# Addend rows through VectorE's block transpose and two GpSimd DMAs, and a layer norm behind the last division, in a two-layer graph network kernel

## The chip, the cores and the metric

One core of one Trainium2 chip. The metric is the device time of one execution in microseconds (us). A time below is a median of runs with the range beside it. All runs told here are of the fast state. The profiled span of a run is 1.7 to 1.9 us shorter than its time (1.86 in the profiled run of the kernel before, 1.76 after), so spans are compared with spans.

## The reference, cut to what matters

64 graphs of 256 nodes with 256 features pass two layers. In the first, each graph goes twice through graph attention, then a layer norm, a feed-forward with 1024 hidden columns and another layer norm:

```python
def _gat(h, adj, W, a, out_features):
    Wh = jnp.matmul(h, W)
    Wh1 = jnp.matmul(Wh, a[:out_features])
    Wh2 = jnp.matmul(Wh, a[out_features:])
    e = Wh1 + jnp.swapaxes(Wh2, 1, 2)
    e = jax.nn.leaky_relu(e, negative_slope=ALPHA)
    scores = jnp.where(adj > 0, e, NEG)
    att = jax.nn.softmax(scores, axis=1)
    return jnp.matmul(att, Wh)
# first layer:  h = _gat(x, adj, W1, a1); h = _gat(h, adj, W2, a2)
#               h = ln(x + h);  ln(h + relu(h @ w_ff1 + b_ff1) @ w_ff2 + b_ff2)
# second layer: 8-head attention with relations, @ Wo + bo, ln(src + .), gelu feed-forward, ln
```

The kernel keeps scores transposed, so `Wh1`, one number per node, is needed as a row that every one of the 128 partitions holds. These are the *addend rows*; four belong to each pair of graphs and layer: two graphs, each with exp(Wh1) and exp(0.2 Wh1).

## The kernel before

Graphs go in 32 pairs. Each pair's work is a generator, and a small scheduler interleaves up to three of them. A `yield us, later, needs` says how long the step was, after how many further us of the scheduler's time the next may follow, and which resource that needs. This sets only the order in which instructions are emitted. The build then re-orders within each engine, so the order on the chip is read from the trace.

```python
def addends(y, at, layer, pair, b):
    ...  # rise = exp(Wh1), exp(0.2 Wh1); ratio = exp(-0.8 Wh2): three ScalarE exponentials a graph
def gat_weights(y, at, rise, ratio, adjT, empty, b):
    p = bank()
    for n in range(4):
        col = rise[:, n // 2, n % 2:n % 2 + 1]
        nc.tensor.transpose(p[:, n * P:(n + 1) * P], col.to_broadcast([P, P]), ident)      # L225
    up = work.tile([P, N], F32, name="up", bufs=2)
    nc.scalar.activation(up, p[:, :N], AF.Copy)                                            # L227
    ...
        nc.vector.scalar_tensor_tensor(e[:, j], p[:, N:], ratio[:, j:j + 1], up, ...)      # L232
        nc.vector.scalar_tensor_tensor(e[:, j], adjT[:, k], empty[:, k:k + 1], e[:, j], ...)  # L233
    nc.vector.reciprocal(rs, sums)
    ...  # ScalarE scales xw by rs (L238)

def attention(y, pair, adjT):
    ...
    def into_rows(b):         # output projection of graph b, reads oT (L427)
        ...
        add_rows(y, ps, b)
        layernorm(y, ln[2], b)
    ...
    for n, (b, c) in enumerate(groups):   # 4 groups: 2 graphs x 2 halves of the heads
        ...
        divided(b, c, po)     # reciprocal of the sums (L416), product into oT (L420)
        yield 3.1 if last else 4.1, 4.8 if last else 0.8, None
        ...
        if n == 2:
            into_rows(0)
            yield 1.75, 0.0, None
    into_rows(1)
```

A layer norm runs on VectorE with one power operation on GpSimd (L302).

Of the kernel before, what the change touches and what calls it, by code (L numbers as in the profile page):

```python
# [29 lines left out]
def two_layers(ctx: ExitStack, tc: tile.TileContext, t: dict, out: bass.AP, flag: bass.AP):  # L30
# [25 lines left out]
    def load(pair):  # L56
        rows = slice(2 * pair, 2 * pair + 2)
        xT = io.tile([P, KC, 512], F32, name="xT")
        nc.sync.dma_start(xT, t["xT"][pair].rearrange("(c p) b n -> p c (b n)", p=P))
        adjT = io.tile([P, 4, N], I32, name="adjT", bufs=4)  # L60
        nc.sync.dma_start(adjT, t["adjT"][rows].rearrange("b (c p) n -> p (b c) n", p=P))
        x = io.tile([P, 4, D], F32, name="x", bufs=4)
        nc.sync.dma_start(x, t["x"][rows].rearrange("b (c p) d -> p (b c) d", p=P))
        return xT, adjT, x

# [8 lines left out]
    nc.vector.memset(ones, 1.0)  # L74
    reach = const.tile([P, NPAIR, 2 * KC], F32, name="reach")
    most = const.tile([P, NPAIR, 4], F32, name="most")
    steep = const.tile([P, NPAIR, 4], F32, name="steep")

    def weights(name, pool=const):
        w = t[name]  # L80
# [62 lines left out]

    work = ctx.enter_context(tc.tile_pool(name="work", bufs=1))
    small = ctx.enter_context(tc.tile_pool(name="small", bufs=6))
    psum = ctx.enter_context(tc.tile_pool(name="psum", bufs=8, space=bass.MemoryType.PSUM))

    def bank():
        return psum.tile([P, 512], F32, name="ps")
# [53 lines left out]
    def of_graph(b):  # L203
        return slice(2 * b, 2 * b + 2)


    def addends(y, at, layer, pair, b):


        k = of_graph(b)  # L210
        nc.vector.tensor_reduce(steep[:, pair, 2 * layer + b:2 * layer + b + 1], y[:, k, at:at + 2], axis=AX.XY,  # L211
                                op=ALU.max, apply_absolute_value=True)
        e1, e2 = y[:, k, at], y[:, k, at + 1]
        rise, ratio = small.tile([P, 2, 2], F32, name="rise"), small.tile([P, 2], F32, name="ratio")
        nc.scalar.activation(rise[:, 0], e1, AF.Exp, bias=shift[:, 0:1])  # L215
        nc.scalar.activation(rise[:, 1], e1, AF.Exp, bias=shift[:, 0:1], scale=ALPHA)
        nc.scalar.activation(ratio, e2, AF.Exp, scale=ALPHA - 1.0)
        return rise, ratio

    def gat_weights(y, at, rise, ratio, adjT, empty, b):  # L220

        p = bank()
        for n in range(4):
            col = rise[:, n // 2, n % 2:n % 2 + 1]
            nc.tensor.transpose(p[:, n * P:(n + 1) * P], col.to_broadcast([P, P]), ident)  # L225
        up = work.tile([P, N], F32, name="up", bufs=2)
        nc.scalar.activation(up, p[:, :N], AF.Copy)  # L227
        e = work.tile([P, 2, N], F32, name="e", bufs=4)
        sums, rs = small.tile([P, 2], F32, name="sums"), small.tile([P, 2], F32, name="rs")
        for j in range(2):  # L230
            k = 2 * b + j
            nc.vector.scalar_tensor_tensor(e[:, j], p[:, N:], ratio[:, j:j + 1], up, op0=ALU.mult, op1=ALU.max)  # L232
            nc.vector.scalar_tensor_tensor(e[:, j], adjT[:, k], empty[:, k:k + 1], e[:, j],  # L233
                                           op0=ALU.max, op1=ALU.min, accum_out=sums[:, j:j + 1])
        nc.vector.reciprocal(rs, sums)
        for j in range(2):
            k = 2 * b + j
            nc.scalar.activation(y[:, k, :at], y[:, k, :at], AF.Copy, scale=rs[:, j:j + 1])  # L238
        return e

    def gat_layers(pair, xT, adjT, x):
        nc.vector.tensor_reduce(most[:, pair], adjT.bitcast(U32), axis=AX.X, op=ALU.max)
        empty = small.tile([P, 4], F32, name="empty")
        nc.vector.tensor_scalar(empty, most[:, pair], 0.0, EVEN, ALU.is_le, ALU.mult)
        y = work.tile([P, 4, D + 4], F32, name="xw", bufs=2)
        z = work.tile([P, 4, D + 4], F32, name="xw", bufs=2)
        a, e = [], []
        for b in range(2):
            for j in range(2):
                k = 2 * b + j  # L250
                ps = bank()
                for c in range(KC):
                    nc.tensor.matmul(ps[:, :D + 4], lhsT=xT[:, c, k * P:(k + 1) * P], rhs=w12[:, c],  # L253
                                     start=c == 0, stop=c == KC - 1)
                nc.scalar.activation(y[:, k], ps[:, :D + 4], AF.Copy)
            a.append(addends(y, D + 2, 0, pair, b))
            yield 1.75, b * 1.6, None
        if pair + 1 < NPAIR:
            loaded[pair + 1] = load(pair + 1)
        for b in range(2):  # L260
            e.append(gat_weights(y, D + 2, *a.pop(0), adjT, empty, b))
            yield 0.5, b * 4.4, None
        for b in range(2):
            for i in range(2):
                ps = bank()
                for j in range(2):
                    nc.tensor.matmul(ps[:, :D + 2], lhsT=e[b][:, j, i * P:(i + 1) * P], rhs=y[:, 2 * b + j, :D + 2],  # L267
                                     start=j == 0, stop=j == 1)
                nc.scalar.activation(z[:, 2 * b + i, :D + 2], ps[:, :D + 2], AF.Copy)  # L269
            a.append(addends(z, D, 1, pair, b))  # L270
            yield 1.75, 0.4 + b * 0.6, None
        for b in range(2):
            e.append(gat_weights(z, D, *a.pop(0), adjT, empty, b))
            yield 0.5, b * 4.4, None
        for b in range(2):
            ps = bank()
            for i in range(2):
                for j in range(2):
                    nc.tensor.matmul(ps[:, i * D:(i + 1) * D], lhsT=e[2 + b][:, j, i * P:(i + 1) * P],  # L279
                                     rhs=z[:, 2 * b + j, :D], start=j == 0, stop=j == 1)  # L280
            add_rows(x, ps, b)
            layernorm(x, ln[0], b)
            if b == 0:
                yield 1.75, 0.4, None
        done_with("gat")
        yield 1.75, 6.0, None
# [80 lines left out]
    def attention(y, pair, adjT):  # L367
# [54 lines left out]
        def into_rows(b):  # L422
            ps = bank()
            for j in range(2):
                k = 2 * b + j
                for c in range(KC):
                    nc.tensor.matmul(ps[:, j * D:(j + 1) * D], lhsT=oT[:, c, k * P:(k + 1) * P], rhs=wo[:, c, :],  # L427
                                     start=c == 0, stop=c == KC - 1)
            add_rows(y, ps, b)
            layernorm(y, ln[2], b)  # L430

        groups = [(b, c) for b in range(2) for c in range(KC)]
        v = values_tile()
# [12 lines left out]
        for n, (b, c) in enumerate(groups):  # L446
            last = n == len(groups) - 1
            if not last:
                ahead = scores(*groups[n + 1])
            po = bank()  # L450
            sums(e, po)
            products(c, 0, v, e, po)
            products(c, 1, v, ms, po)
            if not last:
                e, ms = ahead, of_relation_1(groups[n + 1][0], ahead)
            divided(b, c, po)
            yield 3.1 if last else 4.1, 4.8 if last else 0.8, None
            if n == 0:
                following = values_tile()
                for jc in range(2):  # L460
                    values(following, jc, N + jc * P, yT)
                    yield 1.72, 0.0, None
            if n == 1:
                v = following
            if n == 2:
                into_rows(0)
                yield 1.75, 0.0, None
        into_rows(1)
        done_with("attention")
        yield 1.75, 6.0, None  # L470

    def whole_way(pair):
        yield 0.0, 0.0, "gat"
        xT, adjT, x = loaded.pop(pair)
        yield from gat_layers(pair, xT, adjT, x)
        if pair == 0:
            relieve(ff0[1], ff0[0], ln[0][2])
        yield from feed_forward(x, ff0, AF.Relu, ln[1])
        yield 3.44, 6.0, None
        if pair == 0:  # L480
            relieve_attention(ln[1][2])
        yield from attention(x, pair, adjT)
        if pair == 0:
            relieve(ff1[1], ff1[0], ln[2][2])
        yield from feed_forward(x, ff1, AF.Gelu, ln[3])
        nc.sync.dma_start(out[2 * pair:2 * pair + 2].rearrange("b (c p) d -> p (b c) d", p=P), x)
        yield 3.44, 0.0, None

    in_turn((whole_way(pair) for pair in range(NPAIR)), 3)


    ranges = ((reach, NPAIR * 4, N * SAFE), (most, NPAIR * 4, 1.0), (steep, NPAIR * 4, STEEP))
    count = const.tile([P, len(ranges)], F32, name="count")
    for n, (found, width, most_allowed) in enumerate(ranges):
        kept = const.tile([P, width], F32, name=f"kept{n}")
# [434 lines left out]
```

## Time and profile before

| | before |
|---|---|
| time, median of 3 runs (range) | 3386.12 us (3384.53 to 3388.64) |
| profiled span | 3384.70 us |
| start: span's begin to the first feed-forward matmul | 51.43 us |
| middle: from there to the end of the last matmul | 3324.25 us |
| end: after the last matmul | 9.02 us |

I split the span at two points of TensorE's (PE's) timeline because each stretch has another limit. In the start there is one pair and nobody to fill PE's gaps. In the middle, three pairs are interleaved and PE is the bound. At the end everybody waits for the last layer norm and the last store. The views of this kernel are in the prediction.

### The profile page before, as it was taken

What the parts mean: (1) busy time and instruction counts of PE and PEld (TensorE: products, weight loads), DVE (VectorE), ACT (ScalarE), POOL (GpSimd) and SP (SyncE); (2) the same over time, 40 slices, a digit from 0 to 9 for tenths busy, and PEclk for the clock granted to TensorE, in tenths of its full rate; (3) what the DMA queues carried; (4) which work ended last, traced back from release to release, by engine and by line L of the source; (5) the groups of instructions that cost most, each with busy time, mean ns of one, the idle gap of its engine ahead of it and who ended that gap; (6) DMA issues with size and microseconds to landing.
All of it is one profiled execution on the core that took longest, in us unless ns stands there. A gap on an engine that the chain in (4) does not pass through costs nothing.

```text
span 3384.7 us, 46922 instructions
## 1 busy us (share of the span) xinstructions
PE 3335.3 (99%) x18782; PEld 2161.4 (64%) x18782; DVE 1863.3 (55%) x4833; ACT 1366.4 (40%) x2576; POOL 202.8 (6%) x262
## 2 busy tenths in 40 slices
PE   7999999999999999999999999999999999999998
PEld 5656755765676667557656756676576567665755
DVE  5646556556555555565466556555564565565454
ACT  3234434532353254245433542542354335425332
POOL 0000000000000000000000000000000000000000
PEclk9999999999999999999999999999999999999999
DMA  5000100100010001001000100010010001000000
GB/s 170 7 7 26 38 7 9 43 19 13 15 42 14 7 26 38 7 7 44 19 7 13 38 26 7 26 38 7 7 44 19 7 14 38 20 7 19 13 1 14
DMA packets 67296, 78.19 MB, mean 23 GB/s; under 512 B 3712, under 2 KB 58112, under 8 KB 67072
## 3 DMA queue, kind: packets, MB, share of 16 engines
q1 hardware_dynamic: 67072, 75.13, 7.2%
q8 instruction: 150, 2.46, 0.3%
q14 instruction: 74, 0.61, 0.1%
HBM read 58.34 MB, written 16.78 MB: 22 GB/s over the span
## 4 chain that ended last, share of the span: by engine, by line
PE 95%; ACT 4%; DMA 1%; SPq 0%; issue 0%; DVE 0%; POOL 0%; POOLq 0%; DVEq 0%
PE ps L341 26%; PE ps L330 25%; PE ps L364 7%; PE ps L410 7%; PE ps L357 6%; PE ps L382 4%; PE ps L403 4%; PE ps L253 3%; PE ps L427 3%; PE ps L279 3%; PE ps L317 3%; PE ps L267 2%; ACT L215 2%; PE ps L225 1%; ACT L333 1%; ACT xw L269 1%
## 5 line engine op out<-in xcount | busy, mean ns | idle before, releaser
L319 ACT ACTIVATE yT<-ps 128x512 f32<-128x512 f32 x192 | 113.0, 589 | 1069.7 <-PE ps L317 1069.6
L330 PE MATMUL ps<-yT,w_L_gnn_w_ff 128*128 128x512 f32 x1024 | 480.0, 601 | 0.7 <-ACT yT L319 0.7
L330 PE MATMUL ps<-yT,w_L_gnn_W 128*128 128x512 f32 x1024 | 472.4, 596 | 1.4 <-ACT yT L319 1.4
L341 PE MATMUL ps<-w_L_gnn_w_ff,ff 128*128 128x256 f32 x2048 | 458.2, 381 | 0.0
L341 PE MATMUL ps<-w_L_gnn_W,ff 128*128 128x256 f32 x2048 | 456.8, 380 | 0.0
L341 PEld LDWEIGHTS ps<-w_L_gnn_W,ff 128*128 128x128 f32 x2048 | 388.2, 190 | 65.8 <-issue 14.6
L341 PEld LDWEIGHTS ps<-w_L_gnn_w_ff,ff 128*128 128x128 f32 x2048 | 388.1, 190 | 65.8 <-issue 14.3
L396 DVE TENSOR_TENSOR m<-a,adjT 128x512 f32<-128x512 f32 x512 | 327.2, 687 | 175.4 <-ACT a L387 130.3
L302 POOL TENSOR_TENSOR rstd<-rstd,mhalf 128x2 f32<-128x2 f32 x256 | 202.1, 789 | 3175.3 <-DVE rstd L301 3161.6
L387 ACT ACTIVATE a<-ps 128x512 f32<-128x512 f32 x512 | 264.3, 603 | 232.9 <-PE ps L382 232.8
L359 DVE TENSOR_TENSOR v<-ps,b_L_gnn_bv 128x512 f32<-128x512 f32 x128 | 88.1, 689 | 464.4 <-PE ps L357 464.4
L292 DVE TENSOR_TENSOR x<-ps,x 128x512 f32<-128x512 f32 x256 | 175.8, 687 | 265.2 <-PE ps L341 142.1
L333 ACT ACTIVATE ff<-ps,c_L_gnn_b_ff 128x512 f32<-128x512 f32 x256 | 175.9, 687 | 346.0 <-PE ps L330 346.0
L330 PEld LDWEIGHTS ps<-yT,w_L_gnn_W 128*128 128x128 f32 x1024 | 185.3, 190 | 179.0 <-issue 173.7
L330 PEld LDWEIGHTS ps<-yT,w_L_gnn_w_ff 128*128 128x128 f32 x1024 | 182.1, 190 | 178.9 <-issue 175.9
L333 ACT ACTIVATE ff<-ps,c_L_gnn_b 128x512 f32<-128x512 f32 x256 | 175.7, 686 | 148.3 <-PE ps L330 146.7
L357 PE MATMUL ps<-wv,yT 128*128 128x512 f32 x512 | 235.4, 592 | 0.0
L416 DVE RECIPROCAL s<-ps 128x256 f32<-128x256 f32 x128 | 224.0, 1750 | 0.0
L232 DVE SCALAR_TENSOR_TENSOR e<-ps,ratio,up 128x256 f32<-128x256 f32 x256 | 115.8, 475 | 174.0 <-ACT up L227 174.0
L299 DVE BATCH_NORM_STATS2 st<-x 128x6 f32<-128x256 f32 x512 | 192.7, 418 | 8.7
L357 PEld LDWEIGHTS ps<-wv,yT 128*128 128x128 f32 x512 | 97.3, 190 | 122.4 <-issue 122.4
L211 DVE TENSOR_REDUCE steep<-xw 128x1 f32<-128x4 f32 x128 | 19.7, 155 | 256.8 <-ACT xw L269 211.0
(96 smaller groups left out, 4027.6 us busy)
## 6 DMA issues: line engine op xcount, KB each, us to landing
xT<-in_xT SPq DMA_DIRECT2D x32, 512.0 KB, 4.6
adjT<-in_adjT SPq DMA_DIRECT2D x32, 512.0 KB, 3.8
x<-in_x SPq DMA_DIRECT2D x32, 512.0 KB, 4.2
out<-x SPq DMA_DIRECT2D x32, 512.0 KB, 3.2
w_L_gnn_w_ff<-in_L_gnn_w_ff SPq DMA_DIRECT2D x2, 1024.0 KB, 9.4
w_L_gnn_W<-in_L_gnn_W SPq DMA_DIRECT2D x2, 1024.0 KB, 10.3
wv<-in_L_gnn_Wv SPq DMA_DIRECT2D x2, 256.0 KB, 5.0
w_L_gnn_W1T<-in_L_gnn_W1T SPq DMA_DIRECT2D x1, 256.0 KB, 2.8
```

The lines of the kernel that those rows point to most:

```text
L292: nc.vector.tensor_tensor(rows, p, rows, ALU.add)
L299: nc.vector.bn_stats(st[:, j, :], r[:, 2 * b + j, :])
L302: nc.gpsimd.tensor_tensor(rstd, rstd, mhalf[:, :2], ALU.pow)
L330: nc.tensor.matmul(p1, lhsT=w1[:, c, m * P:(m + 1) * P], rhs=yT[:, c, :], start=c == 0, stop=c == KC - 1)
L333: nc.scalar.activation(h, p1, func, bias=b1[:, m:m + 1])
L341: nc.tensor.matmul(p2[:, j * D:(j + 1) * D], lhsT=f[m][:, k * P:(k + 1) * P], rhs=w2[:, m, :], start=m == 0, stop=m == NF - 1)
L357: nc.tensor.matmul(ps, lhsT=yT[:, c, at:at + P], rhs=wv[:, c].rearrange("p r m -> p (r m)"), start=c == 0, stop=c == KC - 1)
L364: nc.tensor.matmul(ps, lhsT=w[:, d, c * P:(c + 1) * P], rhs=yT[:, d, :], start=d == 0, stop=d == KC - 1)
L387: nc.scalar.activation(a, ps[o], AF.Exp)
L396: nc.vector.tensor_tensor(m, a, adj, ALU.mult)
L410: nc.tensor.matmul(po[o * DH:(o + 1) * DH, :N], lhsT=v[:, jc, at:at + DH], rhs=ms[o][:, jc * N:(jc + 1) * N], start=r == 0 and jc == 0, st ...
L416: nc.vector.reciprocal(s, po[:, N:])
```

## The change

Its intent is to take 512 transposes off PE, the bounding engine. VectorE transposes the exponentials in blocks of 32x32 instead, a small DMA writes the blocks to DRAM as rows, and a second DMA broadcasts the rows to all partitions. Both DMAs are issued by GpSimd. In addition the first graph's layer norm behind attention is emitted after the last division rather than before it, the next pair's load and the store come later, and `x` has five buffers instead of four.

```diff
-    def addends(y, at, layer, pair, b):
+    def addends(y, at, layer, pair):
 ...
+        rise, ratio = rises[layer], small.tile([P, 4], F32, name="ratio")
+        of_kind = rise.rearrange("p j (n s) -> p n j s", n=4)[:, :, :, 0]
 ...
+        blocks = small.tile([P, 2, 32], F32, name="blocks")
+        nc.vector.transpose(blocks.rearrange("p j c -> p (j c)"), rise.rearrange("p j c -> p (j c)"))
+        row = scratch.tile([2, 16, 32], F32, name="row")
+        nc.gpsimd.dma_start(row.rearrange("j q c -> q j c"), blocks[0:P:8])
+        rows = work.tile([P, 8, 4, 32], F32, name="rows")
+        nc.gpsimd.dma_start(rows.rearrange("p q n c -> p (q n c)"), row.rearrange("j q c -> (j q c)").partition_broadcast(P))
 ...
-    def gat_weights(y, at, rise, ratio, adjT, empty, b):
-        p = bank()
-        for n in range(4):
-            col = rise[:, n // 2, n % 2:n % 2 + 1]
-            nc.tensor.transpose(p[:, n * P:(n + 1) * P], col.to_broadcast([P, P]), ident)
-        up = work.tile([P, N], F32, name="up", bufs=2)
-        nc.scalar.activation(up, p[:, :N], AF.Copy)
 ...
+        rows, ratio = addends(y, D + 2, 0, pair)
+        yield 1.75, 8.6, None
+        e = [gat_weights(y, D + 2, rows, ratio, adjT, empty, b) for b in range(2)]
+        yield 0.0, 4.6, None
 ...                                   (the same for the second layer; the load of the next pair moved behind it)
             add_rows(y, ps, b)
-            layernorm(y, ln[2], b)
 ...
             divided(b, c, po)
+            if last:
+                layernorm(y, ln[2], 0)
 ...
         into_rows(1)
+        layernorm(y, ln[2], 1)
```

More of the change, by code (lines that the diff above doesn't have):

```diff
@@ L61, in load @@
         nc.sync.dma_start(adjT, t["adjT"][rows].rearrange("b (c p) n -> p (b c) n", p=P))
-        x = io.tile([P, 4, D], F32, name="x", bufs=4)
+        x = io.tile([P, 4, D], F32, name="x", bufs=5)
         nc.sync.dma_start(x, t["x"][rows].rearrange("b (c p) d -> p (b c) d", p=P))
@@ L76, in two_layers @@
     most = const.tile([P, NPAIR, 4], F32, name="most")
-    steep = const.tile([P, NPAIR, 4], F32, name="steep")
+    steep = const.tile([P, NPAIR, 2], F32, name="steep")
+    rises = [const.tile([P, 2, 32], F32, name=f"rise{n}") for n in range(2)]
+    for rise in rises:
+        nc.vector.memset(rise, 0.0)
     def weights(name, pool=const):
@@ L145, in two_layers @@
     small = ctx.enter_context(tc.tile_pool(name="small", bufs=6))
+    scratch = ctx.enter_context(tc.tile_pool(name="scratch", bufs=4, space=bass.MemoryType.DRAM))
     psum = ctx.enter_context(tc.tile_pool(name="psum", bufs=8, space=bass.MemoryType.PSUM))
@@ L204, in of_graph, with gat_weights @@
         return slice(2 * b, 2 * b + 2)
-    def addends(y, at, layer, pair, b):
-        k = of_graph(b)
-        nc.vector.tensor_reduce(steep[:, pair, 2 * layer + b:2 * layer + b + 1], y[:, k, at:at + 2], axis=AX.XY,
-                                op=ALU.max, apply_absolute_value=True)
-        e1, e2 = y[:, k, at], y[:, k, at + 1]
-        rise, ratio = small.tile([P, 2, 2], F32, name="rise"), small.tile([P, 2], F32, name="ratio")
-        nc.scalar.activation(rise[:, 0], e1, AF.Exp, bias=shift[:, 0:1])
-        nc.scalar.activation(rise[:, 1], e1, AF.Exp, bias=shift[:, 0:1], scale=ALPHA)
-        nc.scalar.activation(ratio, e2, AF.Exp, scale=ALPHA - 1.0)
-        return rise, ratio
-    def gat_weights(y, at, rise, ratio, adjT, empty, b):
-        p = bank()
-        for n in range(4):
-            col = rise[:, n // 2, n % 2:n % 2 + 1]
-            nc.tensor.transpose(p[:, n * P:(n + 1) * P], col.to_broadcast([P, P]), ident)
-        up = work.tile([P, N], F32, name="up", bufs=2)
-        nc.scalar.activation(up, p[:, :N], AF.Copy)
+    def addends(y, at, layer, pair):
+        nc.vector.tensor_reduce(steep[:, pair, layer:layer + 1], y[:, :, at:at + 2], axis=AX.XY, op=ALU.max,
+                                apply_absolute_value=True)
+        rise, ratio = rises[layer], small.tile([P, 4], F32, name="ratio")
+        of_kind = rise.rearrange("p j (n s) -> p n j s", n=4)[:, :, :, 0]
+        for b in range(2):
+            e1 = y[:, of_graph(b), at]
+            nc.scalar.activation(of_kind[:, 2 * b], e1, AF.Exp, bias=shift[:, 0:1])
+            nc.scalar.activation(of_kind[:, 2 * b + 1], e1, AF.Exp, bias=shift[:, 0:1], scale=ALPHA)
+        nc.scalar.activation(ratio, y[:, :, at + 1], AF.Exp, scale=ALPHA - 1.0)
+        blocks = small.tile([P, 2, 32], F32, name="blocks")
[4 more added lines that the diff above has]
+        nc.gpsimd.dma_start(rows.rearrange("p q n c -> p (q n c)"), row.rearrange("j q c -> (j q c)").partition_broadcast(P))
+        return rows, ratio
+    def gat_weights(y, at, rows, ratio, adjT, empty, b):
         e = work.tile([P, 2, N], F32, name="e", bufs=4)
@@ L231, in gat_weights @@
             k = 2 * b + j
-            nc.vector.scalar_tensor_tensor(e[:, j], p[:, N:], ratio[:, j:j + 1], up, op0=ALU.mult, op1=ALU.max)
+            nc.vector.scalar_tensor_tensor(e[:, j].rearrange("p (q c) -> p q c", q=8), rows[:, :, 2 * b + 1],
+                                           ratio[:, k:k + 1], rows[:, :, 2 * b], op0=ALU.mult, op1=ALU.max)
             nc.vector.scalar_tensor_tensor(e[:, j], adjT[:, k], empty[:, k:k + 1], e[:, j],
@@ L246, in gat_layers @@
         z = work.tile([P, 4, D + 4], F32, name="xw", bufs=2)
-        a, e = [], []
         for b in range(2):
@@ L255, in gat_layers @@
                 nc.scalar.activation(y[:, k], ps[:, :D + 4], AF.Copy)
-            a.append(addends(y, D + 2, 0, pair, b))
-            yield 1.75, b * 1.6, None
-        if pair + 1 < NPAIR:
-            loaded[pair + 1] = load(pair + 1)
-        for b in range(2):
-            e.append(gat_weights(y, D + 2, *a.pop(0), adjT, empty, b))
-            yield 0.5, b * 4.4, None
+            if b == 0:
+                yield 1.75, 0.0, None
+        rows, ratio = addends(y, D + 2, 0, pair)
+        yield 1.75, 8.6, None
+        e = [gat_weights(y, D + 2, rows, ratio, adjT, empty, b) for b in range(2)]
+        yield 0.0, 4.6, None
         for b in range(2):
@@ L269, in gat_layers @@
                 nc.scalar.activation(z[:, 2 * b + i, :D + 2], ps[:, :D + 2], AF.Copy)
-            a.append(addends(z, D, 1, pair, b))
-            yield 1.75, 0.4 + b * 0.6, None
-        for b in range(2):
-            e.append(gat_weights(z, D, *a.pop(0), adjT, empty, b))
-            yield 0.5, b * 4.4, None
+            if b == 0:
+                yield 1.75, 0.4, None
+        rows, ratio = addends(z, D, 1, pair)
+        if pair + 1 < NPAIR:
+            loaded[pair + 1] = load(pair + 1)
+        yield 1.75, 8.6, None
+        e += [gat_weights(z, D, rows, ratio, adjT, empty, b) for b in range(2)]
+        yield 0.0, 4.6, None
         for b in range(2):
@@ L485, in whole_way @@
         yield from feed_forward(x, ff1, AF.Gelu, ln[3])
+        yield 3.44, 5.0, None
         nc.sync.dma_start(out[2 * pair:2 * pair + 2].rearrange("b (c p) d -> p (b c) d", p=P), x)
-        yield 3.44, 0.0, None
     in_turn((whole_way(pair) for pair in range(NPAIR)), 3)
-    ranges = ((reach, NPAIR * 4, N * SAFE), (most, NPAIR * 4, 1.0), (steep, NPAIR * 4, STEEP))
+    ranges = ((reach, NPAIR * 4, N * SAFE), (most, NPAIR * 4, 1.0), (steep, NPAIR * 2, STEEP))
     count = const.tile([P, len(ranges)], F32, name="count")
```

## The prediction

> **What bounds the kernel now.** I read the page's busy shares first, then the chain that ended last, then TensorE's (PE's) groups by shape, its waits, and timelines of the middle, the start and the end.
>
> ```profile
> PE 3335.3 (99%) x18782; PEld 2161.4 (64%) x18782; DVE 1863.3 (55%) x4833; ACT 1366.4 (40%) x2576; POOL 202.8 (6%) x262
> ...
> PE 95%; ACT 4%; DMA 1%; SPq 0%; issue 0%; DVE 0%; POOL 0%; POOLq 0%; DVEq 0%
> ```
>
> PE is busy 3335.3 of 3384.7 us, so it has 49.4 us of idle time. The chain that ended last is 95% PE. VectorE is 55% and ScalarE 40% busy. So a change gains what it takes out of PE's stream, plus what it takes out of those 49.4 us, and no more.
>
> The row that the change removes, from PE's groups by shape (busy, mean ns of one | idle before):
>
> ```profile
> L225 PE MATMUL ps<-ident,rise 128*128 128x128 f32 x512 | 71.3, 275 | 19.4 <-ACT rise L215 19.4
> ```
>
> These are the transposes that spread the addend rows over all partitions. 275 ns is not what one costs. In the chain, in order of time (start, us, what), from a busy stretch of the middle:
>
> ```profile
> 1011.06 1.72 PE ps L330 x4
> 1012.78 0.87 PE ps L225 x8
> 1013.65 5.15 PE ps L330 x12
> ```
>
> Eight take 0.87 us of the stream, 109 ns each; the row's 275 is the modelled length of an overlapped instruction. So the transposes hold 512 x 0.109 = 55.8 us. PE's waits complete the account:
>
> ```profile
> PE ps L225 <- ACT rise L215: 19.4, 23, 0.9
> PE pw L117 <- DVE junk L111: 7.3, 1, 7.3
> PE ps L253 <- DMA xT<-in_xT: 5.1, 1, 5.1
> PE ps L279 <- ACT xw L238: 3.3, 1, 3.3
> PE ps L267 <- ACT xw L238: 2.6, 1, 2.6
> ```
>
> The largest wait also belongs to L225: the second graph's transposes find their exponentials unfinished in 23 cases. The idle time counts from a modelled end; one wait in the timeline near the end shows what it costs:
>
> ```profile
> 3169.11 0.60 PE L225 MATMUL ps<-ident,rise 128*128 128x128 f32 x4
> 3170.63 0.65 PE L225 MATMUL ps<-ident,rise 128*128 128x128 f32 x4 [0.92 <-ACT rise L215]
> ```
>
> The stream stood from 3169.11 + 4 x 0.109 = 3169.55 to 3170.63, that is 1.08 us where the note says 0.92. 23 x 0.16 = 3.7 us more makes the waits about 23 us. The other listed waits are single and at the start; from about 52 us on PE idles only before L225. The remainder, 3384.7 - 3375.7 = 9 us, is the final layer norm, store and range check after the last matmul.
>
> **What the Trainium skill says.** (1) "Perfetto Trace Analysis", section Identifying the Most-Contended Engine: matmul occupancy misleads because matmuls are pipelined. The trace agrees: 275 ns recorded, 109 ns of stream. (2) "VectorE: DVE Perf Modes", section The three transpose paths: VectorE transposes 32x32 blocks only, so a row of 256 comes out in pieces, and DMAs must join and broadcast them. No transpose on VectorE is in this trace. (3) "DMA: Bandwidth & Descriptors", section Anatomy of one DMA — SWDGE (gpsimd) path: about 2.0 us plus bytes over 436 GB/s; by it (an estimate) the 512 KB broadcast takes 3.2 us. Here no DMA is issued by GpSimd; SyncE's of 512 KB land in 3.2 us (out) to 4.6 us (xT). I use 4 us. (4) Same page, section Two DMAs through the same engine are not ordered: the issuing engine must wait for the first DMA's semaphore before the second. So GpSimd's queue stands still between the two. No run yet shows it.
>
> **The change part by part.**
>
> *Transposes and row copies out.* PE loses 55.8 us of stream and the 23 us of waits. ScalarE loses L227 (128 x 379 ns = 42 us) and some exponentials: per layer and pair five activations instead of six. Neither is on the path. Four PSUM-bank uses per pair go too, and PE waits for none today.
>
> *Addend rows in.* Per layer and pair (64 times): one 128x64 VectorE transpose (estimate 0.2 us, from 0.16 us for the small VectorE operations here and 0.42 for 256 columns), a DMA of 16 blocks x 256 B to DRAM, and a 512 KB broadcast back. The L232 operations stay 256, reading SBUF instead of PSUM; L233, same size and from SBUF, takes 477 ns against 475, so nothing changes. VectorE gains 64 x 0.2 = 13 us and loses 64 reductions of 155 ns = 10 us. The added traffic, 64 x 0.5 MB = 34 MB, is 10 GB/s beside 23.
>
> *Latency.* From the last projection: copy 0.4, four exponentials 1.2 (a table load of 1.28 in some cases), transpose 0.2, first DMA with GpSimd's issue about 3, second about 4.5: 9 to 11 us. Then VectorE needs 2 x (0.48 + 0.48 + 0.08) = 2.1 us a graph and ScalarE 2 x 0.5 us before the product.
>
> I stepped the source's scheduler with the diff's yields, for the order of instructions only. Its delays are 8.6 + 4.6 us, and its steady order puts between 15 and 35 of its microseconds, nearly all of them other pairs' PE work, between the end of the projections and the product. So the latency is covered, with 4 us or more to spare. GpSimd's held queue can delay one layer norm per pair (power at L302) by some 2 us, but its reader, a PE transpose, comes 4 to 8 us later. I allow 2 us in all.
>
> *The start.* Pair 0 has nobody beside it:
>
> ```profile
> 15.35 0.62 PE L225 MATMUL ps<-ident,rise 128*128 128x128 f32 x4
> 16.28 0.65 PE L225 MATMUL ps<-ident,rise 128*128 128x128 f32 x4 [0.31 <-ACT rise L215]
> 19.56 3.75 PE L267 MATMUL ps<-xw,e 128*128 128x258 f32 x16 [2.62 <-ACT xw L238]
> ...
> 38.56 5.38 PE L253 MATMUL ps<-w,xT 128*128 128x260 f32 x16 [5.10 <-DMA xT<-in_xT]
> ...
> 51.43 1.22 PE L330 MATMUL ps<-yT,w_L_gnn_w_ff 128*128 128x512 f32 x1 [0.69 <-ACT yT L319]
> ```
>
> From the projections' end (15.4) to the first product took 4.1 us; it will take about 13.5. The product then lies at 29; the second graph's follows 2 us later and ends near 34. The same again puts the second layer's products at 47 to 51, pair 1's projections (today held by xT until 38.56) at 51 to 55, and the first L330 9 steps later at 51.43 - 38.56 + 51 = 64 instead of 51.4. That shift of 12.5 us is net of the 5.1 us xT wait, which vanishes. DMA queues are full until 44 us (340 to 360 GB/s), so DMAs may be slower; PE's clock is lowered after such gaps (granted 0.87 in the mean from 12 to 52 us by the windows view, 1.00 after), perhaps no worse than today. Another 2 us falls in thin places of the new order before 110 us.
>
> *Layer norm behind the last division, later load and store, fifth x buffer.* The norm (about 4 us of VectorE) leaves the way of the last division (2.7 us), but no wait on the reader L427 is listed today. The tail has the same idle places as before. Worth 0.
>
> **The sum.** Profiled span 3384.7 - 55.8 - 23 + 12.5 + 2 + 2 = 3322.4. The 12 startup transposes before the first L330 and their three waits are counted in both terms: 12 x 0.109 + 1.5 = 2.8. Timed runs lie 1.4 us above the span (3386.12): 3326.6. My DMA times at the start are cautious, so I choose **3325 us**, -1.8%.
>
> **Rivals.**
> A: *The wait moves to VectorE.* If the round trip takes 15 us or more, VectorE stands in order at L232 and holds back attention's masking, and PE waits. For: VectorE is strictly in order, and the GpSimd path is unmeasured. Against: 8.6 us of planned delay and 7 or more behind it. At 1 us per layer and pair it costs 64 us, and the time is about 3388.
> B: *GpSimd's queue holds up the layer norms.* For: VectorE already waits 149.9 us in 256 cases for L302, and one norm per pair falls between the two DMAs. Against: the slack above. At 1 us a pair, 32 us: 3356.
> C: *The start is hidden better.* PE has waits for xT there anyway. If both round trips end in 10 us rather than 13.5, the start costs 5 instead of 12.5: 3316, over 2%.
> D: *ScalarE's fewer exponentials save table loads that matter.* 69 loads of 1283 ns stand at L215 today, but only the 23 waits, already counted, reach PE. Worth 0 to 3 us.
>
> **Range and chances.** PE's removed stream is certain to a few microseconds; the start can be 7 us better or 10 worse, and steady-state stalls add 0 to 15 us. That gives 3313 to 3340. The 2% limit is 3386.12 x 0.98 = 3318.4, 7 us below my figure and inside C: 0.24 faster, 0.75 same, 0.01 slower.
>
> **What would show it.** Right: L225 and L227 gone; PE waits on nothing after the first 110 us; first L330 near 64 us; PE's busy time down by about 71 us (the modelled 275 ns each); POOL showing two DMAs per layer and pair, landing within 3 and 4.5 us of issue. Wrong: PE waits on L238 or on the layer norm's reader in the middle, VectorE idle at L232's successor while PE waits too, a first L330 before 57 or after 72 us, or a granted clock in the middle below 1.0.

## The result and the profile after

The changed kernel takes **3347.56 us** (3344.81 to 3350.42, 5 runs); the kernel before took 3386.12 (3384.53 to 3388.64, 5 runs) beside it. The ratio is 0.9886 with a 95% interval of 0.9872 to 0.9899. (Ratios here and below are the mean time of one kernel's fast runs over that of the other's of the same rounds, so not quite the ratio of the quoted medians.) It is 1.1% faster, within 2% as I had thought likeliest, but 22.6 us over my 3325 and 7.6 us over the upper end of my range.

| stretch, us of the span | before | after | moved | predicted |
|---|---|---|---|---|
| start | 51.43 | 72.59 | +21.2 | +12.5 |
| middle | 3324.25 | 3257.43 | -66.8 | -72.0 (-55.8 -23 +2 +2 +2.8) |
| end | 9.02 | 14.47 | +5.5 | 0 |
| sum | 3384.70 | 3344.49 | -40.2 | -59.5 |

The three misses, 8.7, 5.2 and 5.5 us, make 19.4. The other 3.2 us of the 22.6: I chose 1.6 below my own sum, counted 1.4 instead of 1.76 between span and time after the change, and the profiled run lies 1.3 below the median.

The busy shares (busy us, share, instructions) and the chain that ended last, by engine, from the page after:

```profile
PE 3283.8 (98%) x18270; PEld 2106.0 (63%) x18270; DVE 1836.8 (55%) x4835; ACT 1263.6 (38%) x2326; POOL 275.7 (8%) x390
...
PE 94%; DMA 3%; DVE 2%; ACT 1%; issue 0%; POOL 0%; SPq 0%; POOLq 0%; DVEq 0%
```

There are 18782 - 18270 = 512 matmuls fewer. A DMA share of 3% is new in the chain, where 1% stood. PE's waits after (total us, times, longest):

```profile
PE ps L274 <- ACT xw L247: 18.3, 1, 18.3
PE ps L289 <- ACT xw L247: 14.2, 1, 14.2
...
PE ps L437 <- DVE oT L430: 0.2, 1, 0.2
```

The 19.4 us wait in 23 cases is gone. The first two lines are single waits, both of pair 0: for the product of each graph-attention layer, where the kernel before waited 2.6 and 3.3. They are the start's loss: 26.6 us more than the two waits before, less the 5.1 us wait for xT that went, is 21.5. Its chain in order of time (start, us, what):

```profile
24.06 8.90 DMA rows<-row
...
35.83 5.51 PE ps L274 x16
...
42.30 0.26 DVE blocks L227
...
42.83 5.19 DMA row<-blocks
...
48.57 4.09 DMA rows<-row
...
55.52 5.86 PE ps L289 x16
```

In the first layer the block transpose stood at 18.55, the write was issued at 19.10 and the broadcast at 24.06, and VectorE's first reader of the rows began at 33.07: 14.5 us. In the second it is 42.30 to 52.76, 10.5 us. Over all 64 cases, nearly all of them in the middle, the same two transfers land in a median of 1.9 and 3.9 us, by the page's list of DMA issues (KB each, us to landing):

```profile
rows<-row POOLq DMA_DIRECT2D x64, 512.0 KB, 3.9
...
row<-blocks POOLq DMA_DIRECT2D x64, 4.0 KB, 1.9
```

Where the end's 5.5 us went is in the instructions of the kernel's last line, of kind DRAIN on GpSimd (min/median/max ns, first and last start). Before, then after:

```profile
L926 POOLq DRAIN  x3: 34/45/82, 3379.0 to 3384.3; - x3
```

```profile
L938 POOLq DRAIN  x3: 40/107/10522, 3333.2 to 3344.2; - x3
```

One DRAIN takes 10.5 us, from 3333.2 to 3343.7, and the span ends at 3344.5. The last store is issued at 3333.97 and has landed by 3338.44 in the trace, so this drain outlasts it.

For the middle I compared one pair's second output projection in both. PE's timeline and VectorE's, before (start, us, engine, line, what):

```profile
1405.38 1.05 PE L410 MATMUL ps<-m,v 128*32 128x256 f32 x16
...
1413.37 1.89 PE L427 MATMUL ps<-w_L_gnn_Wo,oT 128*128 128x256 f32 x8
```

```profile
1410.93 0.42 DVE L420 TENSOR_TENSOR oT<-ps,s 128x256 f32<-128x256 f32 x1
```

And after:

```profile
1354.08 1.05 PE L420 MATMUL ps<-m,v 128*32 128x256 f32 x16
...
1361.16 2.22 PE L437 MATMUL ps<-w_L_gnn_Wo,oT 128*128 128x256 f32 x8
```

```profile
1361.35 0.42 DVE L430 TENSOR_TENSOR oT<-ps,s 128x256 f32<-128x256 f32 x1
```

Before, the division's result was ready at 1411.35, two us ahead of the projection. After, it is ready at 1361.77 when the projection has begun at 1361.16, and the eight matmuls take 2.22 us instead of 1.89. That is a wait of 0.33 us which the list of waits does not show. Summed over all pairs by the starts of these matmuls, it is 3.9 us after and 0.0 before.

### The profile page after: what moved, and what is told of

The parts are those of the page before. It is cut to its first block, busy times and chain, and to the rows that moved or that the text cites. A ratio compares the mean times of both kernels' runs of the same rounds, so it can differ in the third digit from the quotient of the medians.

```text
span 3344.5 us, 45688 instructions
## 1 busy us (share of the span) xinstructions
PE 3283.8 (98%) x18270; PEld 2106.0 (63%) x18270; DVE 1836.8 (55%) x4835; ACT 1263.6 (38%) x2326; POOL 275.7 (8%) x390
## 4 chain that ended last, share of the span: by engine, by line
PE 94%; DMA 3%; DVE 2%; ACT 1%; issue 0%; POOL 0%; SPq 0%; POOLq 0%; DVEq 0%
PE ps L351 26%; PE ps L340 25%; PE ps L420 6%; PE ps L367 6%; PE ps L374 6%; PE ps L392 4%; PE ps L413 4%; PE ps L289 4%; PE ps L261 3%; PE ps L437 3%; PE ps L274 3%; PE ps L327 2%; DMA rows<-row 1%; DMA adjT<-in_adjT 1%; DMA row<-blocks 1%; DVE e L240 0%
## 5 line engine op out<-in xcount | busy, mean ns | idle before, releaser
L340 PE MATMUL ps<-yT,w_L_gnn_w_ff 128*128 128x512 f32 x1024 | 452.7, 595 | 0.7 <-ACT yT L329 0.7
L340 PEld LDWEIGHTS ps<-yT,w_L_gnn_w_ff 128*128 128x128 f32 x1024 | 192.8, 191 | 218.1 <-issue 208.2
L240 DVE SCALAR_TENSOR_TENSOR e<-rows,ratio 128x256 f32<-128x256 f32 x256 | 116.3, 477 | 322.7 <-DMA rows<-row 314.8
L247 ACT ACTIVATE xw<-xw,rs 128x258 f32<-128x258 f32 (+1 forms) x256 | 117.4, 502 | 144.0 <-DVE rs L244 144.0
```

The lines of the kernel that those rows point to most:

```text
L340: nc.tensor.matmul(p1, lhsT=w1[:, c, m * P:(m + 1) * P], rhs=yT[:, c, :], start=c == 0, stop=c == KC - 1)
```

## The experiments

My theory had four parts: the start pays for round trips under a full load of DMAs; the end pays for GpSimd's drain; the middle's shortfall comes from short waits in the new order; and the moved norm is worth nothing. Each had a rival.

### The start: pair 0 by the old way

```diff
+        if pair == 0:   # addends_pe, gat_weights_pe: the transposes of the kernel before
+            ... a.append(addends_pe(y, D + 2, 0, pair, b)); yield 1.75, b * 1.6, None
+            ... e.append(gat_weights_pe(y, D + 2, *a.pop(0), adjT, empty, b)); yield 0.5, b * 4.4, None
+        else:
             rows, ratio = addends(y, D + 2, 0, pair)
```

> The changed kernel, but pair 0 alone spreads its addends by TensorE transposes as the kernel before did. If the start is the largest part of what I missed (first L330-type matmul at 72.6 us after the change against 51.4 before), the first feed-forward matmul comes back to 51 to 53 us, the middle and the end stay as in the changed kernel (3257 and 14.5 us), and the time falls by about 20 us to 3327 (3323 to 3331). Rival: the start is only shifted and the first pairs give it back later, or the loss lies in the middle; then the time stays within 6 us of 3347.5.

Measured: 3323.38 us (3322.08 to 3324.27), ratio to before 0.9812 (0.9796 to 0.9828), correct. The first feed-forward matmul comes at 49.39 us, the middle takes 3258.70, the end 14.33. So the start's loss lies wholly in pair 0's two round trips: giving back 16 transposes won some 23 us.

### The start: fewer loads in the way

Why were the trips 14.5 and 10.5 us? Two kernels keep the change and hold back loads. The first holds 3.6 MB of second-layer weights until pair 0's second broadcast has landed; the second also holds the first feed-forward weights (2 MB) and the next pairs' loads until its first broadcast has landed.

```diff
+        if after is not None:
+            nc.vector.tensor_copy(s[:, 0, 0:1], after)   # writes one column, so the load must wait for it
         nc.sync.dma_start(s, w.rearrange("(c p) m -> p c m", p=P))
```

> The changed kernel with seven weight loads that nobody needs before 110 us (about 3.6 MB: attention's four matrices and the second feed-forward's two) held back until pair 0's second row broadcast has landed, each by one small VectorE copy into its tile. If the start is slow because the addend DMAs share full DMA engines with these loads, the two round trips fall from 14 and 10 us (write issued to rows used) towards the 7 us of the middle, the first feed-forward matmul comes at 62 to 67 us instead of 72.6, and the time is 6 to 10 us shorter, 3337 to 3342. Rival: the trips are slow for another reason (TensorE's halved clock, other VectorE work ahead); then it stays within 3 us of 72.6 us and 3347.

> As quiet_start, and in addition the first feed-forward weights (2 MB) and the loads of the next pairs are held until the first pair's first broadcast has landed, so that nothing but small vectors and the first pair's own tiles is moving when the first round trip starts. Theory (the queue full of loads delays the first trip too): write issue to broadcast issue falls from 6.3 us (quiet_start) to about 2 to 3 us and the landing from 7 to 4 to 5 us, TensorE's wait at the first product falls from 17.3 us to 8 to 11 us, and the first feed-forward matmul comes at 58 to 63 us if the held weights land in time. Rival (the first trip is long for another cause, such as the first use of GpSimd's queue): the two intervals stay within 1 us of those of quiet_start although the DMA share has fallen below half there, and the wait stays at 16 us or more.

Measured, holding the second-layer weights (quiet_start): 3344.55 us (3344.29 to 3348.44), ratio 0.9881, first feed-forward matmul at 68.67. Holding more (quieter_start): 3341.96 (3341.29 to 3345.13), ratio 0.9874, first feed-forward matmul at 63.91. The first hold freed the second trip only. Its chain:

```profile
25.68 6.63 DMA rows<-row
...
42.74 1.61 DMA row<-blocks
44.91 3.83 DMA rows<-row
```

The second hold freed the first trip, and its released loads now fell on the second:

```profile
19.33 2.90 DMA row<-blocks
22.79 3.99 DMA rows<-row
...
36.87 5.07 DMA row<-blocks
42.49 3.81 DMA rows<-row
```

The DMA share in the stretches with the trips (from, to | ... | PE's granted clock, DMA share, GB/s at the end of the line), for the second hold:

```profile
20.00:27.00 7.00, 0.00 (x0) 0.00 (x0) 0.62 (x3) 0.00 (x0) 0.59 (x2) 0.71 0.39 121
...
34.00:42.00 8.00, 1.36 (x7) 0.84 (x5) 1.80 (x4) 1.85 (x8) 0.52 (x1) 0.87 1.08 355
```

(The view adds up the time of packets, so a share can come out above 1.) At a share of 0.39 the broadcast took 3.99 us, at 1.08 the write took 5.07. Taken over exactly the time of each transfer, the share was 0.02, 0.61, 1.09 and 1.03 for the writes of 1.61, 2.90, 5.07 and 5.74 us in the two holds, and 0.40, 0.41 and 0.62 for the broadcasts of 3.99, 3.83 and 6.63; the changed kernel's 8.90 us had 0.80. One does not fit: the second hold's second broadcast took 3.81 us at 0.71. So the same transfer is slow or quick with the load on the DMA engines, the write in every case and the broadcast in all but one, and a first-use cost is not needed to explain it. That agrees with the Trainium skill, "DMA: Bandwidth & Descriptors", section Issuing engines are not separate DMA queues: DMAs end up on the same 16 engines and interleave whichever engine issued them. My figures for the new starts were somewhat too good: 68.67 where I expected 62 to 67, since the first hold left the first trip under load, and 63.91 where I expected 58 to 63: the first product still waited 12.3 us instead of 8 to 11, and the released loads hit the second trip. The times fell by 3.0 and 5.6 us (I had expected 6 to 10 of the first hold), less than the starts, because the middle grew by 2.0 and 4.5 us.

### The end: who issues, and how many

Three kernels: the changed one with both addend DMAs on SyncE's queue; the changed one with only the broadcast on SyncE's; and the kernel before with one small DMA from GpSimd.

```diff
-        nc.gpsimd.dma_start(row..., blocks[0:P:8])      # sp_queue only
+        nc.sync.dma_start(row..., blocks[0:P:8])
-        nc.gpsimd.dma_start(rows..., row....partition_broadcast(P))   # sp_queue and write_pool_read_sp
+        nc.sync.dma_start(rows..., row....partition_broadcast(P))
```

```diff
+    once = const.tile([P, 4], F32, name="once")         # one_pool_dma, on the kernel before
+    nc.gpsimd.dma_start(once, t["x"][0, :P, :4])
```

> The changed kernel with both addend DMAs issued by SyncE instead of GpSimd. Theory: the 10.5 us DRAIN of GpSimd's queue after the last matmul, 0.05 us before the change, comes from its having issued DMAs; then it falls to under 0.2 us, the stretch after the last matmul goes from 14.5 to about 9 us, and the time falls by 5 us to about 3342 if the round trip is not longer. Rival: the longer end comes from the later store of the output (its yield was moved); then the end stays near 14.5 us. Second question: SyncE's queue now waits between the two DMAs and holds loads and stores; if that mattered, TensorE would wait for xT or x, which I do not expect.

> The changed kernel with the 4 KB write left on GpSimd's queue and the 512 KB broadcast issued by SyncE. One GpSimd DMA left the final DRAIN at 0.14 us, 124 made it 10.2 and 128 made it 10.5 us, which is 82 ns each. If it counts DMAs, 64 of them give 5.3 us and the end is about 9 us (the store takes 4 to 5 us beside it), time 3342. If it counts what they move or their packets (128 rows of 4 KB against 32 blocks of 128 B each), the DRAIN is under 2.5 us. Second: GpSimd's queue no longer waits for the write to land, so its powers are never held behind it.

> The kernel before with one added 2 KB DMA issued by GpSimd during set-up, read by nobody. Theory: having issued any DMA makes GpSimd's final DRAIN take about 10 us, a fixed cost; then the end after the last matmul goes from 9.0 to about 14.5 us and the time rises by 5 us to about 3391. Rival: the DRAIN grows with the number of DMAs issued (128 in the changed kernel); then one DMA leaves it under 0.5 us and the time stays at 3386.

| kernel | DMAs from GpSimd | longest DRAIN of the last line, us | end, us |
|---|---|---|---|
| both on SyncE (sp_queue) | 0 | 0.08 | 8.87 |
| one small DMA (one_pool_dma) | 1 | 0.14 | 9.35 |
| broadcast on SyncE (write_pool_read_sp) | 64 | 5.30 | 9.70 |
| pair 0 the old way (first_pair_pe) | 124 | 10.20 | 14.33 |
| after | 128 | 10.52 | 14.47 |

```profile
L938 POOLq DRAIN  x3: 44/107/5300, 3334.3 to 3340.5; - x3
```

The drain grows by 0.082 us with each DMA that GpSimd issued (10.52 / 128 and 5.30 / 64 give 0.082 and 0.083). It goes by the number and not the bytes: the 64 writes of 4 KB cost half of what 64 writes and 64 broadcasts of 512 KB do. A fixed price for using GpSimd's queue at all, which I had thought possible, fell with the single DMA: 3386.97 us, ratio 1.0002. Only what outlasts the last store counts, which is why 5.30 us of drain cost 0.7 us of time at the end: there the store has landed at 3338.64 and the drain ends at 3339.64.

With both DMAs on SyncE the time is 3342.29 us (3339.57 to 3347.24, ratio 0.9869). The end won its 5.6 us, but part of that was lost because the start rose to 75.74: there the first write was issued at 30.77 instead of 19.10, since SyncE's queue issues in order and its weight loads stood in front. With only the broadcast on SyncE it was 3343.47 us (3339.86 to 3345.03, ratio 0.9873).

### The norm: put back, and moved alone

`ln_back` is the changed kernel with the norm before the last division again; `ln_only` is the kernel before with the norm's move and nothing else.

```diff
 ln_back:                                       ln_only, on the kernel before:
+            layernorm(y, ln[2], b)            -            layernorm(y, ln[2], b)
-            if last:                          +            if last:
-                layernorm(y, ln[2], 0)        +                layernorm(y, ln[2], 0)
-        layernorm(y, ln[2], 1)                +        layernorm(y, ln[2], 1)
```

> The changed kernel with the first graph's layer norm put back before the last division: one part undone. Theory: the layer norm was never on the path, so the time is that of the changed kernel within 4 us (3344 to 3351). Rival: the move pays; without it TensorE waits for the last division before the second output projection (L437-type) and the time is 10 us or more longer. Third possibility: the move costs, and the small waits of L437 for oT (some 0.1 to 0.3 us a pair) go, 3 to 5 us faster.

> The kernel before with only the layer norm moved behind the last division. In the kernel before TensorE has no wait at the second output projection, so the move alone should bring nothing: 3386 (3383 to 3390), no wait of L427 for oT in either. Rival: the move is worth 44 us by itself, as the run with the norm put back could suggest; then about 3342.

Measured: put back, 3391.98 us (3390.56 to 3394.21), ratio 1.0018 (1.0001 to 1.0035). The whole gain of the change was gone, where I had expected no more than 4 us; this was the study's surprise. Moved alone: 3387.08, ratio 1.0001 (0.9986 to 1.0017), no effect. Put back, PE's waits begin with a line that neither kernel has:

```profile
PE ps L437 <- DVE oT L430: 40.3, 30, 2.2
```

and one pair of its middle, on PE and VectorE, reads

```profile
1371.50 1.05 PE L420 MATMUL ps<-m,v 128*32 128x256 f32 x16
...
1378.58 0.59 PE L437 MATMUL ps<-w_L_gnn_Wo,oT 128*128 128x256 f32 x2
1380.95 1.56 PE L437 MATMUL ps<-w_L_gnn_Wo,oT 128*128 128x256 f32 x6 [1.78 <-DVE oT L430]
```

```profile
1380.48 0.42 DVE L430 TENSOR_TENSOR oT<-ps,s 128x256 f32<-128x256 f32 x1
```

The last division's result is ready at 1380.90, its reader stands from 1378.58 + 2 matmuls. Two things moved against each other here. From the start of the last product to the second output projection PE has 1413.37 - 1405.38 = 7.99 us of work in the kernel before, and 1361.16 - 1354.08 = 7.08 in the new order. And VectorE finishes the division 1411.35 - 1405.38 = 5.97 us after that product's start before, but 1380.90 - 1371.50 = 9.40 when the norm stands in front of it in the new order, because there VectorE begins the whole norm behind the last product (its first add at 1373.03), where in the kernel before its add and statistics are done by then. Before, the margin was 2.0 us, so nothing was to be gained from the move. In the new order it is -2.3 us with the norm in front, and -0.6 us (1361.77 against 1361.16, of which the first two matmuls cover half) with the norm moved. The norm is emitted behind the division then, but the trace shows only its last part there: VectorE still does the add, the statistics and part of the scaling first. What left the division's way is above all the wait for GpSimd's power (0.58 us) and the norm's last two operations (0.88 us): the division ends 1361.77 - 1354.08 = 7.69 us after the product's start instead of 9.40. The move is a necessary part of the change: 3388.79 - 3344.49 = 44 us of span.

### The order without the DMAs

Were the 23 us of waits at the transposes a matter of the transposes or of the order? This kernel has the changed kernel's order and yields, the norm behind the division, and the old transposes for every pair. (One more difference to the kernel before: the copy `up` has one buffer instead of two.)

```diff
-        rows, ratio = addends(y, D + 2, 0, pair)
+        a = [addends_pe(y, D + 2, 0, pair, b) for b in range(2)]
         yield 1.75, 8.6, None
-        e = [gat_weights(y, D + 2, rows, ratio, adjT, empty, b) for b in range(2)]
-        yield 0.0, 4.6, None
+        e = [gat_weights_pe(y, D + 2, *a[b], adjT, empty, b) for b in range(2)]
+        yield 0.87, 4.6, None
```

> The changed kernel's order (norm behind the last division, its yields), but every pair's addends by TensorE transposes as in the kernel before: the transposes come back, the round trip through GpSimd's queue and its end drain go. My theory: the sum of the middle had two terms, 55.8 us for the transposes themselves and 23 us for TensorE's waits at them, and the waits were a matter of the order, not of the transposes. Then the first feed-forward matmul comes at about 51 us, the middle takes 3257.4 + 504 x 0.109 = about 3312 us, the end 9 us, the time is 3370 to 3376, and TensorE's waits at the transposes add up to under 8 us. Rival: the waits belong to the transposes wherever they stand, or their place is taken by the wait of the second output projection for the scaled projection; then the waits in the middle sum to over 15 us and the time is 3384 or more.

Measured: 3378.62 us (3375.35 to 3381.77), ratio 0.998 (0.9965 to 0.9995); start 47.30, middle 3318.61, end 8.93. The waits at the transposes fell from 19.4 to 0.7 us, so they did belong to the order:

```profile
PE ps L266 <- ACT rise L257: 0.7, 2, 0.4
```

But the middle came out 6.6 us above the 3312 I expected, and the time above my 3370 to 3376. Part of that is a new wait:

```profile
PE ps L359 <- DVE x L350: 7.0, 7, 1.2
```

These seven waits for a layer norm all fall in about the last third, where a pair takes 104.38 us in the mean instead of 103.42. So of the 38.6 us that the whole change won, the new order alone brings about 7 (by the interval of the ratio, 2 to 12).

The steady period of 103.42 us a pair also re-measures the transposes: the second kernel of the next section has the same order apart from a delay, no transposes after pair 0, and 101.51. The difference, 1.91 us for 16 transposes, is 0.119 us each, against the 0.109 that I had read from the chain.

### Putting it together

Two kernels collect what was found: pair 0 by the old way *and* the remaining addend DMAs on SyncE; and the same with more feed-forward matmuls ahead of the second output projection (in the trace 32 stand there instead of 16).

```diff
-            yield 3.1 if last else 4.1, 4.8 if last else 0.8, None
+            yield 3.1 if last else 4.1, 6.4 if last else 0.8, None      # best_slack only
```

> Both parts that the first runs showed costly undone together: pair 0 by TensorE transposes, and the DMAs of all other pairs issued by SyncE. If the start (21 to 24 us) and GpSimd's final DRAIN (5.5 us) are separate costs they add up: first feed-forward matmul near 50 us, end after the last matmul near 9 us, time 3318 (3315 to 3321), 2.0% under the kernel before. Rival: SyncE's queue, now held while the first pairs load, gives part of it back; then 3322 or more.

> The fastest version so far (first pair by TensorE transposes, the other addend transfers from SyncE, 3317) with the last attention group's delay 4.8 -> 6.4, so that eight more feed-forward matmuls stand ahead of the second output projection. Theory: the small waits of TensorE there, 0.1 to 0.3 us a pair for the scaled projection, are most of what the middle fell short of its ideal of 101.62 us a pair; then the middle goes from 3258.4 to 3253 to 3256 us and the time to 3312 to 3315. Rival: the shortfall sits in other waits or only moves along; then the time stays at 3317 within 1 us.

Measured: the first takes **3317.34 us** (3316.36 to 3318.55), ratio 0.9795 (0.9782 to 0.9809), with 49.21 / 3258.42 / 9.14 us for the stretches. The second takes **3312.72 us** (3310.46 to 3318.79), ratio 0.9789 (0.9776 to 0.9803), with 46.89 / 3252.67 / 9.13. Both are correct and beat both kernels; whether by the full 2% is not settled, since both intervals include 0.98. Against each other they ran in different sessions and their ranges overlap, so I don't call the second faster by its time. Its profile does show the small wait gone: the eight matmuls after the slack are as long as in the kernel before,

```profile
1338.48 1.89 PE L488 MATMUL ps<-w_L_gnn_Wo,oT 128*128 128x256 f32 x8
```

their sum of lengthening is 0.0 us where the first had 4.5, and pairs follow each other at exactly 101.51 us for eighteen steady periods, where the first had 101.76 in the mean of the same eighteen. In the last third both stand at 101.91. PE is never idle there, and the matmuls are the same but interleaved differently. The record shows where most of those 0.4 us a pair go. In every one of these pairs, in both kernels, one group of four transposes behind a layer norm is longer, here in the second:

```profile
2857.39 0.85 PE L378 MATMUL ps<-ident,x 128*128 128x128 f32 x4
```

In the steady part it takes 0.60. It starts 0.10 us late, and its second transpose's weights start to load at 2857.69, just after VectorE's last operation of the norm has ended at 2857.64. So 0.3 us is another wait that the list leaves out; the last 0.1 stays open.

## Why the prediction was right or wrong

**The transposes, -55.8: right.** 512 are gone, and 0.119 us each by the comparison of periods would make 61. My sign for it, PE's busy time down by 71 us, was badly chosen: 275 ns records overlap their neighbours, and busy time counts the union. (71.3 us is the union of the group by itself; 512 x 275 ns would be 141.) It fell by 51.5.

**The waits at them, -23: right in sum, wrong in cause.** They are gone after the change. But they would also have gone with the transposes in place, by the order alone, as the kernel with the new order shows (19.4 to 0.7). The size fits: the kernel before takes 104.06 us a pair in its steady part, the new order 103.42, and 0.64 x 32 makes 20 us (an estimate). The correction for what both terms count was misread: 24 transposes stand before the first L330, pair 0's 16 and pair 1's 8, not 12, so it is 4.1 us and not 2.8.

**The start, +12.5: mis-sized, measured +21.2.** The step that failed is "first DMA with GpSimd's issue about 3, second about 4.5". I did write that DMA queues are full until 44 us, "so DMAs may be slower", called my times cautious, and even subtracted something for it. The mechanism was right and the term was too small: from transpose to rows it took 14.5 and 10.5 us instead of 7.7, together 9.6 us more, where the start missed by 8.7. (The loads were not as even as I wrote either: before the change the DMAs moved 331 to 379 GB/s from 30 to 44 us, but 164 to 171 from 22 to 30, at a share of 0.82 to 0.98.) With fewer loads in the way the first trip took 18.78 to 26.80 = 8.0 us, which is nearly what I had assumed; so the assumption fits the middle of the run, and was applied to the one place where it doesn't hold. I had also written that PE's clock would be lowered "perhaps no worse than today". It was worse: 0.77 in the mean over the first 73 us against 0.90 over the first 52, and the first layer's 16 products took 5.50 us where they had taken 3.75. The Trainium skill, "TensorE: Matmul & The Clock Gate", section Part 1: The HAM clock gate (the "warmup" mystery), has an idle array at half rate; the trace after agrees with a granted clock of 0.50 from 27 to 34 us, where PE does nothing. The sign I had set for being wrong, a first feed-forward matmul after 72 us, came true at 72.59.

**The end, "the tail has the same idle places as before", 0: wrong, measured +5.5.** I looked for compute at the end and not for what GpSimd must do before a program may stop. The drain after 128 DMAs is the term that was missing.

**The thin places and steady stalls, +2 and +2: the middle fell 5.2 us short.** My mark that PE would wait on nothing after the first 110 us nearly held in the list of waits, and the list hid the rest. Some 3.9 us are the lengthened output projections, shown by their vanishing with more slack. The 0.4 us a pair of the last third are mostly the short wait for a layer norm, read from the trace and not tested by a run.

**The norm behind the last division, "worth 0": right for the kernel before, wrong for the change.** Alone it is worth nothing (ratio 1.0001), as I argued from its missing wait. I drew the conclusion from the old order, though the change was about to shorten PE's work in front of the reader and to shift VectorE's. In the new order it is worth 44 us. It did not spoil the sum, because the change contains it.

**The rivals.** A, the wait moving to VectorE, did not come: VectorE does idle for the rows (314.8 us in 55 cases, 293.1 us and 53 of them after the start), but after the start PE's list of waits has none for what follows. B, GpSimd's queue holding up norms, did not come either: VectorE's waits for GpSimd's power are 141.2 us after and 149.9 before, though the queue stood for its own first DMA for 131.0 us in 63 cases. C was the wrong way round. Of D, the table loads at the exponentials did fall from 69 to 28, but to 26 in the kernel with the new order alone, so they belong to the order; what they were worth to PE is not shown.

## What to carry to other kernels

A latency that the steady state hides is paid in full by the first iteration, at the price that it has there: size it from transfers in the loaded start, or let the first iteration go another way. Count the DMAs that GpSimd issues and look at the drain on the kernel's last line when it is moved there. And a move that is worth nothing in the old order can be what carries the new one: before calling a part worthless, recompute the margin at its reader for the order that the change makes.

## What the Trainium skill lacked or had wrong

- No page has the cost at the end of a kernel of DMAs issued by GpSimd; it would belong to "DMA: Bandwidth & Descriptors". Measured: a DRAIN of 0.14, 5.30, 10.20 and 10.52 us after 1, 64, 124 and 128 of them, 0.082 us each and independent of size; none of it with the same DMAs on SyncE's queue.
- "DMA: Bandwidth & Descriptors", section Anatomy of one DMA — SWDGE (gpsimd) path, gives one duration for a size and no term for other traffic on the same DMA engines. The page says that HBM access takes longer at high load, but not what a DMA between others then takes. Its estimate for the 512 KB broadcast is 3.2 us; measured were 3.9 in the median, and 6.6 and 8.9 us under the loads of the start. Its 2.0 us for a small one agrees with the median (1.9 us for 4 KB); at a DMA share of about 1.1 it was 5.1 us.
- "Perfetto Trace Analysis", section Identifying the Most-Contended Engine, warns of matmul occupancy, and the page says that a matmul's end is estimated. It does not say that a wait within a group of matmuls can therefore be absent from a list of waits: here 3.9 us over the run showed almost only as eight matmuls taking up to 2.33 us instead of 1.89.
